# First two token pairs side by side, and the first attention products with their operand sums on GpSimd and TensorE's order written out

## The chip, the cores and the metric

The kernel runs on one core of one Trainium2 chip. The time is the device time of one execution in microseconds (us), lower is better; the kernel before took 1184.9 us in the median of three runs (1184.69 to 1185.73). The engines go by the profile's names: PE is TensorE (matmuls; PEld are its weight loads), DVE is VectorE, ACT is ScalarE, POOL is GpSimd, SP is the engine that issues the DMAs.

## The reference

The reference is one transformer layer on 1024 tokens (4 sequences of 256) of 512 features, all in float32:

```python
x = x + 0.5 * ffn(layernorm(x), A, B, Wr)
x = x + attn(layernorm(x), wq, wkv, wo)
x = x + 0.5 * ffn(layernorm(x), A, B, Wr)

# ffn: 64 experts of rank 16, gated by the softmax of the 16 best scores
scores = xf @ Wr.T
top_vals, top_idx = jax.lax.top_k(scores, 16)
h = jnp.einsum('nd,krd->nkr', xf, A)
out = jnp.einsum('nkr,kdr->nd', h * G[:, :, None], B)
# attn: 32 heads of width 128, causal
scores = jnp.einsum('bqhd,bkhd->bhqk', q[..., :128], k) * 192 ** -0.5
attn = jnp.einsum('bhqk,bkhd->bqhd', softmax(masked(scores)), v)
```

## The kernel before

Every large product is cut into 2 x 2 blocks and done with seven block products where plain multiplication has eight (Strassen-Winograd). The left and the right operands are first summed: `left_sums` (lines 166 to 175) and `right_sums` (177 to 187) make four sums each. `seven` (189 to 198) runs the products M1 to M7 in the order of a list, `STEPS` or `STEPS_LATE` (143 to 159). Several products add up in one PSUM bank, and after each product `read` takes a bank's state out, by ACT (a copy) or by DVE (an add). A product that adds to a bank waits until the earlier state has been read.

**First layer** (`ffn`, lines 239 to 431). It works on four pairs of 128-token tiles. A pair is prepared in three steps (`prepare`, 276 to 310): normalise (DVE statistics L103, ACT L106 to L120); transpose on PE (L127), copy out on ACT (L285) and sum on DVE (L171 to L174); the router's scores on PE (L302) and the gates on DVE and ACT (L249 to L273). Then come seven hidden products on PE (L318, one pair of 128x512 matmuls each, in the trace four instructions), the gating on POOL (`gated`, L345), the transposes of the gated result (`turned`, L364) and seven products back (L384) that DVE adds to `x` (L396). The right operand of the hidden products is the expert matrix A, which comes by DMA in four blocks; M1, M2 and M3 take raw blocks, M5 a sum of DVE (L181), M6 another of DVE (L184), M7 and M4 the sums of POOL (L185, L186). Pair 0 runs `STEPS_LATE`, which puts the raw blocks first. Pair 1 is prepared while pair 0's products run.

**Attention.** Its Q, K and V products use the scheme twice, an outer and an inner level: 7 x 7 = 49 products. The operand `xop[:, outer, inner]` (line 445) holds the normalised, transposed tokens and all their sums. `norm_pair` (457 to 489) fills outer blocks 0 and 1 from pairs 0 and 1, and the raw parts of 2 to 6 from pairs 2 and 3; `inner_sums` (450 to 456) makes the four inner sums of an outer block, each 128x256. The weights' sums are made on POOL by `two_levels` (505 to 535); two of them, `t3` and `t4` (L518, L521, 128x896), turn the sums for the outer M1 and M2 into those for M7 and M4, and may run only after the last matmul that reads the old ones. A *stage* is one outer product or two at a time: seven inner steps on PE (L607 for Q and K, `pqk_*`; L696 for V, `pv_*`), with eight read-outs, by ACT (L627, L727) or by DVE (L625, L637, L645, L721).

For the first head pair, `make_qk(0)` (lines 594 to 675) and the first V stages (`v_stages`, 685 to 766) run as follows: lines 898 to 915 take V and Q/K steps in turn, stage M1, then M2, then V's M6 with a Q/K stage of M6 and M5 together; between them the last token pair's part of `norm_pair` is taken, and the inner sums of outer blocks 5, 4 and 3 go to DVE, those of 2 and 6 to POOL. A memset of POOL (L664) clears a buffer of Q/K ahead. Then the loop over head pairs runs (from line 946): a *unit* is one head and one sequence: scores on PE (`ps`, L834, L835), masking and least value on DVE (L843), exponentials on ACT (L854), DVE (L862), ACT (L864), and one unit later the transposes (L875) and the product with V (L880, L887). The strings `FIRST_UNITS` to `LAST_UNITS` (line 942 on) say which steps are taken behind each unit's scores: `f` of the first Q/K, `g` of the first V stages, `q` of the next head pair's Q/K, `v` of V, `b` the rest of the unit before.

**What sets the order.** Instructions are traced in the order of the Python code; a scheduler then lays out each engine's queue at compile time, from that order as a priority and from when it takes operands to be ready. [...] `tc.keep_in_program_order(i)` holds an instruction behind everything traced before it on its engine. The DMAs of SP go in the order of its queue.

## Time and profile before

| what | value |
|---|---|
| three timed runs, median | 1184.9 us |
| the profiled execution, its own time | 1187.66 us |
| its span, first to last instruction | 1185.5 us |
| PE busy | 1166.3 us, 98% of the span, 6492 matmuls |
| DVE, ACT, POOL busy | 741.7, 492.7, 676.3 us |
| PE busy in 0 to 20 us | 17.18 us |
| PE busy in 20 to 36 us, granted clock | 14.25 us, 0.89 |
| PE busy in 130 to 150 us, granted clock | 17.68 us, 1.00 |
| PE busy in 150 to 166 us, granted clock | 9.90 us, 0.79 |
| PE busy in 176 to 400 us, granted clock | 224.00 us, 1.00 |

The first layer covers 0 to about 130 us, the attention about 130 to 1066 us, the second feed-forward layer the rest. A row of the timeline has its start, its duration, the engine, the source line, the operation, output<-input and the number of instructions merged; square brackets give the idle time ahead and what ended it. A row of the waits names the engine and line that waited, what it waited for, the total in us, the number of times and the longest. A float32 matmul of the program shows as two instructions. Busy time of PE is modelled at its ends, so a loss of PE is better read from the starts of its instructions: at full clock they follow each other every 0.43 us for 128x512, 0.215 us for 128x256 and 0.11 us for 128x128.

### The profile page before, as it was taken

The numbers are of one execution on the slowest core, as the hardware profiler recorded it, in microseconds if no ns is written. First come the engines' busy times: TensorE is split into PE (matmuls) and PEld (weight loads), VectorE is DVE, ScalarE is ACT, GpSimd is POOL, SyncE is SP. The second block draws the span as 40 slices with busy tenths as digits, with TensorE's granted clock in tenths as the row PEclk, the third lists the DMA queues.
The fourth block names the chain that finished last, engine by engine and source line by source line (L and its number), as shares of the span: only waits on it lengthen the run. The fifth ranks groups of instructions, "written<-read, shape, count | busy, mean of one in ns | idle before, by whom it ended". The sixth has DMA issues, their size and how long they took to land.

```text
span 1185.5 us, 18545 instructions
## 1 busy us (share of the span) xinstructions
PE 1166.3 (98%) x6492; PEld 1005.8 (85%) x6492; DVE 741.7 (63%) x1932; ACT 492.7 (42%) x1364; POOL 676.3 (57%) x933
## 2 busy tenths in 40 slices
PE   8999979999999999999999999999999999999998
PEld 5677869999999999999999898989898988875767
DVE  5444786566666666666576657665766666675432
ACT  4443314534443444344434443444443444546420
POOL 5611666986847684667575757657575644361110
PEclk9999989999999999999999999999999999999999
DMA  7001111111001101110111011110201000400001
GB/s 253 1 1 36 45 36 46 28 45 47 27 28 49 50 19 45 37 45 19 46 37 46 28 36 37 45 46 18 63 23 41 19 27 1 161 1 1 19 18 35
DMA packets 64940, 47.46 MB, mean 40 GB/s; under 512 B 4432, under 2 KB 55632, under 8 KB 64848
## 3 DMA queue, kind: packets, MB, share of 16 engines
q1 hardware_dynamic: 64848, 46.28, 13.2%
q8 instruction: 51, 0.84, 0.3%
q14 instruction: 41, 0.34, 0.1%
HBM read 44.17 MB, written 2.10 MB: 39 GB/s over the span
## 4 chain that ended last, share of the span: by engine, by line
PE 95%; DVE 2%; DMA 1%; ACT 1%; issue 0%; POOL 0%; SPq 0%; DVEq 0%; ACTq 0%
PE po L812 16%; PE pqk_c L607 8%; PE po_f L384 8%; PE pqk_a L607 8%; PE pqk_b L607 8%; PE ph_f L318 7%; PE pa L880 5%; PE ps L835 5%; PE pv_c L696 4%; PE pqk_d L607 4%; PE pv_b L696 4%; PE ptp L875 4%; PE ps L834 2%; PE pa L887 2%; PE pv_a L696 2%; PE pv_d L696 2%
## 5 line engine op out<-in xcount | busy, mean ns | idle before, releaser
L824 DVE TENSOR_TENSOR x<-x,po 128x512 f32<-128x512 f32 x224 | 153.9, 688 | 73.6 <-PE po L812 71.4
L854 ACT ACTIVATE s<-s,least 128x128 f32<-128x128 f32 (+1 forms) x256 | 114.5, 448 | 89.7 <-DVE least L843 89.7
L877 ACT COPY pT<-ptp 128x384 f32<-128x384 f32 x128 | 61.3, 479 | 207.6 <-PE ptp L875 207.6
L654 POOL TENSOR_TENSOR qk<-qk 128x256 f32<-128x256 f32 x128 | 92.7, 728 | 67.7 <-DVE qk L645 34.0
L864 ACT ACTIVATE s<-s,arden 128x128 f32<-128x128 f32 (+1 forms) x256 | 102.5, 448 | 51.5 <-DVE arden L862 51.2
L607 PE MATMUL pqk_a<-xop,wqk_M 128*128 128x256 f32 x448 | 116.9, 385 | 0.0
L607 PE MATMUL pqk_c<-xop,wqk_M 128*128 128x256 f32 x448 | 114.3, 381 | 0.0
L843 DVE CUSTOM_DVE_ANT_0 s<-ps,mask 128x128 f32<-128x128 f32 (+1 forms) x256 | 81.5, 356 | 51.0 <-PE ps L835 50.9
L345 POOL TENSOR_TENSOR hg_f<-hg_f,gate_f 128x512 f32<-128x512 f32 x32 | 33.6, 1057 | 132.1 <-DVE hg_f L331 68.9
L607 PE MATMUL pqk_b<-xop,wqk_M 128*128 128x256 f32 x420 | 106.9, 380 | 0.0
L645 DVE TENSOR_TENSOR qk<-qk,pqk_c 128x512 f32<-128x512 f32 x112 | 76.9, 688 | 43.0 <-PE pqk_c L607 33.8
L607 PEld LDWEIGHTS pqk_c<-xop,wqk_M 128*128 128x128 f32 x448 | 81.1, 191 | 9.7 <-DVE qk L645 1.0
L637 DVE TENSOR_TENSOR qk<-qk,pqk_b 128x512 f32<-128x512 f32 x105 | 72.2, 687 | 25.1 <-PE pqk_b L607 24.8
L181 POOL TENSOR_TENSOR wo<-wo 128x256 f32<-128x256 f32 x16 | 11.7, 728 | 128.0 <-DMA wo<-in_wo 112.6
L607 PEld LDWEIGHTS pqk_a<-xop,wqk_M 128*128 128x128 f32 x448 | 78.7, 194 | 6.5
L894 ACT COPY attn<-pa 128x256 f32<-128x256 f32 x128 | 47.5, 371 | 87.5 <-PE pa L887 87.5
L607 PEld LDWEIGHTS pqk_b<-xop,wqk_M 128*128 128x128 f32 x420 | 72.9, 191 | 6.1
L835 PE MATMUL ps<-qk 128*128 128x256 f32 x256 | 76.5, 381 | 0.0
L880 PE MATMUL pa<-pT,vbuf 128*128 128x256 f32 x256 | 76.2, 379 | 0.0
L812 PE MATMUL po<-wo,so 128*128 128x256 f32 x256 | 66.8, 383 | 1.7 <-DVE so L171 1.7
L812 PE MATMUL po<-to,attn 128*128 128x256 f32 x256 | 66.2, 381 | 0.9 <-DVE x L824 0.9
L607 PE MATMUL pqk_d<-xop,wqk_M 128*128 128x256 f32 x224 | 66.3, 380 | 0.0
(193 smaller groups left out, 2784.0 us busy)
## 6 DMA issues: line engine op xcount, KB each, us to landing
wv_M<-in_wkv SPq DMA_DIRECT2D x64, 128.0 KB, 2.5
wqk_M<-in_wq SPq DMA_DIRECT2D x64, 128.0 KB, 2.3
wqk_M<-in_wkv SPq DMA_DIRECT2D x64, 128.0 KB, 2.4
wo<-in_wo SPq DMA_DIRECT2D x16, 512.0 KB, 4.1
a_f<-in_a_t SPq DMA_DIRECT2D x8, 512.0 KB, 6.5
b_f<-in_b_t SPq DMA_DIRECT2D x4, 1024.0 KB, 8.8
x<-in_x SPq DMA_DIRECT2D x8, 256.0 KB, 8.2
out_x<-x SPq DMA_DIRECT2D x16, 128.0 KB, 1.7
```

Of the source, the lines that this page charges most:

```text
L318: nc.tensor.matmul(ps, lhsT=left[m][:, c, :], rhs=a_right[m][:, c, :], start=first and c == 0, stop=c == 1, skip_group_check=True,)
L384: nc.tensor.matmul(ps[:, 0:256], lhsT=left[m][:, c, :], rhs=b_right[m][:, c, :], start=first and c == 0, stop=c == 3, skip_group_check=True,)
L607: nc.tensor.matmul(ps[:, i * S : (i + 1) * S], lhsT=right[m][n], rhs=xop[:, OUTER[m], INNER[n]], start=first and i == 0, stop=True, skip_g ...
L654: nc.gpsimd.tensor_tensor(to, a, b, ALU.add)
L696: nc.tensor.matmul(ps[:, i * S + t * P : i * S + (t + 1) * P], lhsT=xop[:, OUTER[m], INNER[n], t * P : (t + 1) * P], rhs=right[m][n], star ...
L812: nc.tensor.matmul(ps[:, tt * 256 : (tt + 1) * 256], lhsT=outs[p][m][:, (2 * u + tt) * P : (2 * u + tt + 1) * P], rhs=right[m], start=firs ...
L824: nc.vector.tensor_tensor(to, to, ps.rearrange("p (t d) -> p t d", t=2), ALU.add)
L835: nc.tensor.matmul(ps[:, P : 3 * P], lhsT=qT[:, P : 2 * P], rhs=kT, start=True, stop=True)
L843: nc.vector.tensor_tensor_reduce(out=s[:, cols], in0=ps[:, cols], in1=mask_f[:, cols], scale=-SCALE, scalar=-TAKEN, op0=ALU.add, op1=ALU.m ...
L854: nc.scalar.activation(s[:, cols], s[:, cols], AF.Exp, bias=least[:, i : i + 1], scale=-1.0, accum_out=den[:, i : i + 1],)
L864: nc.scalar.mul(s[:, cols], s[:, cols], rden[:, i : i + 1])
L880: nc.tensor.matmul(po[:, 0 : 2 * P], lhsT=v_of(p, j, 2 * b), rhs=pT[:, 0 : 2 * P], start=True, stop=False,)
```

## The change

Seven edits, all before 200 us of the program:

1. The DMAs of the first layer: token tiles 2 and 3 are loaded between the second and the third block of A, tiles 4 to 7 behind the fourth (before: all six behind the fourth).
2. Pair 1 of the first layer is normalised, transposed and takes its first three hidden products ahead of pair 0's last four; both pairs use `STEPS_LATE`, pair 1 with M6 ahead of M5. POOL's sums of B are traced ahead of the gating of pair 0, and the gating of pairs 0 and 1 is pinned in program order.
3. POOL's sums of the first V weights are pinned behind the gating of pair 1 (`aside`).
4. The statistics of the last token pair are taken after two steps of the first V and Q/K stages, its transposes after seven.
5. All inner sums of outer blocks 2 to 6 and the last outer sums (before: two DVE adds, L484 and L485) go to POOL, pinned, in a fixed order with `t3` and `t4`.
6. The first Q/K: stages M1, M2, M6, then M4 with M7, M5 and M3. No memset of POOL.
7. From the first Q/K stage to the end of head pair 0, PE's queue is in the order of the code (`manual_schedule`), with new `FIRST_UNITS`.

The diff, cut to its core; left out are the arguments that pass `pinned` on to `two_levels`, `right_sums` and `left_sums`, and the returned instructions of `t3` and `t4`.

```diff
@@ -220,11 +228,11 @@
...
-        for kn in ((0, 0), (1, 0), (1, 1), (0, 1)):
+        for i, kn in enumerate(((0, 0), (1, 0), (1, 1), (0, 1))):
             c, e = a_block(*kn)
             nc.sync.dma_start(a_sb[:, c, e], a_v[:, c, e])
-        if between is not None:
-            between()
+            if between is not None and i % 2:
+                between(i // 2)
         for k in range(2):
@@ -334,20 +343,22 @@
...
-                steps = STEPS_LATE if late and pair == pairs[0] else STEPS
+                steps = STEPS_LATE if late and pair in pairs[:2] else STEPS
+                if late and pair == pairs[1]:
+                    steps = [steps[i] for i in (0, 1, 2, 4, 3, 5, 6)]
                 yield from seven(product, read, f"ph_{n}", steps)
-            def gated(hg, gate):
+            def gated(hg, gate, pinned):
                 ek = E // 2
...
                         to = hg[:, i, j * 512 : (j + 1) * 512].rearrange("p (e r) -> p e r", r=R)
-                        nc.gpsimd.tensor_tensor(
-                            to,
-                            to,
-                            gate[i][:, j * ek : (j + 1) * ek].unsqueeze(2).to_broadcast([P, ek, R]),
-                            ALU.mult,
+                        of = gate[i][:, j * ek : (j + 1) * ek].unsqueeze(2)
+                        made = nc.gpsimd.tensor_tensor(
+                            to, to, of.to_broadcast([P, ek, R]), ALU.mult
                         )
+                        if pinned:
+                            tc.keep_in_program_order(made)
@@ -402,13 +413,30 @@
...
             yield
-            take(tokens, 2)
+            take(tokens, 1)
+            if late:
+                second = prepare(pairs[1])
+                take(second, 1)
+            take(tokens, 1)
             a_right = a_sums()
             for u in range(n + 1):
-                hid = hidden(pairs[u], lefts[u], hgs) if u < n else iter(())
+                if u == 1 and late:
+                    hid = ahead
+                else:
+                    hid = hidden(pairs[u], lefts[u], hgs) if u < n else iter(())
                 tokens = prepare(pairs[u + 1]) if u + 1 < n else iter(())
                 behind = after(work, pairs[u - 2]) if u > 1 else iter(())
-                take(hid, 1)
+                if u == 0 and late:
+                    take(hid, 3)
+                    take(second, 1)
+                    ahead = hidden(pairs[1], lefts[1], hgs)
+                    take(ahead, 3)
+                    take(hid, 1)
+                    take(second, 1)
+                    tokens = iter(())
+                else:
+                    take(hid, 1)
                 take(behind, 1)
@@ -420,14 +448,17 @@
...
                 take(hid, 3)
-                if u < n:
-                    gated(hgs[pairs[u]], gated_by[u])
                 if u == 0:
                     b_right = b_sums()
+                if u < n:
+                    gated(hgs[pairs[u]], gated_by[u], late and u < 2)
+                if u == 1 and aside is not None:
+                    aside()
                 if u > 0:
...
                     take(steps, 8)
+        yield
         yield from after(None, pairs[n - 1])
@@ -447,12 +478,19 @@
...
-    def inner_sums(lo, hi, eng):
+    def inner_sums(lo, hi, eng, between=None):
         o = slice(lo, hi)
...
             blocks[2] = early
-        left_sums(eng, [xop[:, o, i] for i in (4, 5, 6, 2)], *blocks)
+        left_sums(eng, [xop[:, o, i] for i in (4, 5, 6, 2)], *blocks, pinned=lo > 0, between=between)
+    def last_outer():
+        for of, i in ((early[:, 1], 2), (xop[:, 1, 3], 3)):
+            tc.keep_in_program_order(
+                nc.gpsimd.tensor_tensor(xop[:, 6, i], of, xop[:, 5, i], ALU.subtract)
+            )
@@ -480,15 +518,12 @@
...
                 nc.scalar.copy(xop[:, 0:2, sl, cols], pt)
-        if half and a:
-            nc.vector.tensor_tensor(xop[:, 6, 2], early[:, 1], xop[:, 5, 2], ALU.subtract)
-            nc.vector.tensor_tensor(xop[:, 6, 3], xop[:, 1, 3], xop[:, 5, 3], ALU.subtract)
-        elif half:
+        if half and not a:
             nc.vector.tensor_tensor(xop[:, 6, sl], xop[:, 1, sl], xop[:, 5, sl], ALU.subtract)
-        elif a:
+        elif a and not half:
             inner_sums(0, 2, nc.vector)
-    raw, rights, outs = {}, {}, {}
+    raw, rights, outs, turns = {}, {}, {}, {}
@@ -557,15 +595,25 @@
...
                 ],
+                k == 1,
             )
+    def sums_v(k, pinned=False):
+        rights["v", k] = raw["v", k](**({"pinned": True} if pinned else {}))
+        return rights["v", k]
...
         experts = load_experts(
-            scope, "f1", "right", nc.vector, lambda: load_x(range(2, NT))
+            scope, "f1", "right", nc.vector, lambda i: load_x(range(4, NT) if i else (2, 3))
         )
...
         first_layer = ffn(
-            "f1", [(t, t + 1) for t in range(0, NT, 2)], *experts, after=norm_pair, late=True
+            "f1",
+            [(t, t + 1) for t in range(0, NT, 2)],
+            *experts,
+            after=norm_pair,
+            late=True,
+            aside=lambda: sums_v(0, True),
         )
@@ -642,10 +691,22 @@
...
                 to = part(blocks, r)
-                nc.vector.tensor_tensor(to, to, ps, ALU.add)
+                of = ps if ps.shape == to.shape else ps.to_broadcast(to.shape)
+                nc.vector.tensor_tensor(to, to, of, ALU.add)
                 done(r, into)
...
             return read
+        def m47(r, ps):
+            both, one, two, base = (part(slice(*k), r) for k in ((1, 3), (1, 2), (2, 3), (3, 4)))
+            if READS[r][2]:
+                nc.vector.tensor_tensor(both, both, ps, ALU.add)
+            else:
+                nc.scalar.copy(one, ps[:, 0:1])
+                nc.vector.tensor_tensor(two, base, ps[:, 1:2], ALU.add)
+            if r in LAST:
+                nc.gpsimd.tensor_tensor(one, one, two, ALU.add)
@@ -660,13 +721,16 @@
...
         else:
-            nc.gpsimd.memset(dst[:, 2], 0.0)
-            yield from stage(("M1",), fresh(slice(1, 2)), "m")
-            t3()
-            yield from stage(("M2",), branch(slice(0, 1)), "n")
-            t4()
-            yield from stage(("M6", "M5"), onto(slice(1, 3), 3), "a")
+            turns["qk"] = t3, t4
+            yield from stage(("M1",), fresh(slice(3, 4)), "m")
+            yield from stage(("M2",), branch(slice(0, 1), of=slice(3, 4)), "n")
+            yield from stage(("M6",), onto(slice(3, 4)), "o")
+            yield from stage(("M4", "M7"), m47, "r")
+            yield from stage(("M5",), onto(slice(2, 4)), "s")
+            load_qk(p + 1)
+            yield from stage(("M3",), onto(slice(3, 4)), "u")
+            return
         yield from stage(("M7", "M3"), onto(slice(1, 4, 2), 2), "c")
@@ -895,24 +962,31 @@
...
     load_qk(0)
+    written_out = ExitStack()
+    written_out.enter_context(tc.manual_schedule(engines={mybir.EngineType.PE}))
     first_qk = make_qk(0)
     first_v = chain(*(v_by[0][m] for m in ("M1", "M2", "M6", "M4M7")))
-    for _ in range(7):
-        take(first_v, 1)
-        take(first_qk, 1)
+    def first_products(n):
+        for _ in range(n):
+            take(first_v, 1)
+            take(first_qk, 1)
+    first_products(2)
     take(first_layer, 1)
-    for _ in range(7):
-        take(first_v, 1)
-        take(first_qk, 1)
-    inner_sums(5, 6, nc.vector)
-    inner_sums(4, 5, nc.vector)
+    first_products(5)
+    take(first_layer, 1)
+    tc.keep_in_program_order(turns["v"][0]())
+    tc.keep_in_program_order(turns["qk"][0]())
+    first_products(7)
+    inner_sums(5, 6, nc.gpsimd, last_outer)
+    tc.keep_in_program_order(turns["v"][1]())
     inner_sums(2, 3, nc.gpsimd)
+    inner_sums(3, 4, nc.gpsimd)
+    tc.keep_in_program_order(turns["qk"][1]())
+    inner_sums(4, 5, nc.gpsimd)
     inner_sums(6, 7, nc.gpsimd)
-    for _ in range(7):
-        take(first_v, 1)
-        take(first_qk, 1)
-    inner_sums(3, 4, nc.vector)
-    take(first_qk, 7)
+    first_products(7)
@@ -939,7 +1013,16 @@
...
     )
-    FIRST_UNITS = ("gfgfbgf", "gfgfbgfgf", "gvqvqbvqvq", "vqvqbvqvqvq", "vqvqbvqvqvq", "vqvqbvqq", "vqvqbqvqq", "vqvqbvqqq")
+    FIRST_UNITS = (
+        "gggg",
+        "gggfffbfffffvfvfvfv",
+        "fvfvfvbfvfvfvf",
+        "fvfvbfvfv",
+        "qqvqbqqvq",
+        "qqvqbqqvq",
+        "qqvqbqqvq",
+        "qqvqbqqvq",
+    )
     LAST_UNITS = ("", "b", "oob", "oob", "oob", "oob", "ooob", "ooob")
@@ -977,6 +1060,7 @@
...
             take(streams[k], 100)
+        written_out.close()
         sums_o(p)
```

More of the change, by code (lines that the diff above doesn't have):

```diff
@@ L164, in macaron_kernel, with left_sums @@
     LAST = (3, 4, 5, 6)
-    def left_sums(eng, s, a11, a12, a21, a22, *of):
+    def left_sums(eng, s, a11, a12, a21, a22, *of, pinned=False, between=None):
         s3 = s[3] if len(s) > 3 else a21
         r11, r12, r21, r22 = of or (a11, a12, a21, a22)
-        eng.tensor_tensor(s[0], r21, r22, ALU.add)
-        eng.tensor_tensor(s[1], s[0], r11, ALU.subtract)
-        eng.tensor_tensor(s[2], r12, s[1], ALU.subtract)
-        eng.tensor_tensor(s3, r11, r21, ALU.subtract)
+        for to, a, b, op in (
+            (s[0], r21, r22, ALU.add),
+            (s[1], s[0], r11, ALU.subtract),
+            (s[2], r12, s[1], ALU.subtract),
+            (s3, r11, r21, ALU.subtract),
+        ):
+            if to is s3 and between is not None:
+                between()
+            made = eng.tensor_tensor(to, a, b, op)
+            if pinned:
+                tc.keep_in_program_order(made)
         return {"M1": a11, "M2": a12, "M3": s[2], "M4": a22, "M5": s[0], "M6": s[1], "M7": s3}
@@ L237, in load_experts, with ffn @@
         )
-    def ffn(name, pairs, a_sums, b_sums, after, late):
+    def ffn(name, pairs, a_sums, b_sums, after, late, aside=None):
         with ExitStack() as scope:
@@ L344, in gated @@
                         to = hg[:, i, j * 512 : (j + 1) * 512].rearrange("p (e r) -> p e r", r=R)
-                        nc.gpsimd.tensor_tensor(
-                            to,
-                            to,
-                            gate[i][:, j * ek : (j + 1) * ek].unsqueeze(2).to_broadcast([P, ek, R]),
-                            ALU.mult,
-                        )
+                        of = gate[i][:, j * ek : (j + 1) * ek].unsqueeze(2)
+                        made = nc.gpsimd.tensor_tensor(
+                            to, to, of.to_broadcast([P, ek, R]), ALU.mult
+                        )
+                        if pinned:
+                            tc.keep_in_program_order(made)
             def turned(pair, hg):
@@ L503, in sums_o, with two_levels @@
         rights["o", p] = right_sums(nc.gpsimd, [t[:, i, :] for i in range(3)], *b, pinned=p == 0)
-    def two_levels(pool, bufs, name, blocks):
+    def two_levels(pool, bufs, name, blocks, pinned):
         t = {
@@ L517, in t3, with sums @@
         def t3():
-            nc.gpsimd.tensor_tensor(t["M1"], t["M6"], t["M1"], ALU.subtract)
+            return nc.gpsimd.tensor_tensor(t["M1"], t["M6"], t["M1"], ALU.subtract)
         def t4():
-            nc.gpsimd.tensor_tensor(t["M2"], t["M2"], t["M6"], ALU.subtract)
-        def sums():
+            return nc.gpsimd.tensor_tensor(t["M2"], t["M2"], t["M6"], ALU.subtract)
+        def sums(pinned=pinned):
             plain = {m: v[:, 0:4] for m, v in t.items()}
-            nc.gpsimd.tensor_tensor(plain["M5"], plain["M5"], plain["M1"], ALU.subtract)
+            first = nc.gpsimd.tensor_tensor(plain["M5"], plain["M5"], plain["M1"], ALU.subtract)
+            if pinned:
+                tc.keep_in_program_order(first)
             nc.gpsimd.tensor_tensor(plain["M6"], plain["M3"], plain["M5"], ALU.subtract)
@@ L547, in load_qk @@
                 ],
+                p == 1,
             )()
@@ L629, in fresh, with branch @@
             return read
-        def branch(blocks, into=None):
+        def branch(blocks, into=None, of=slice(1, 2)):
+            base = of
             def read(r, ps):
                 to = part(blocks, r)
-                of = to if READS[r][2] else part(slice(1, 2), r).to_broadcast(to.shape)
+                of = to if READS[r][2] else part(base, r).to_broadcast(to.shape)
                 nc.vector.tensor_tensor(to, of, ps, ALU.add)
@@ L688, in v_stages @@
             return {}
-        right, t3, t4 = raw["v", k]()
+        right, t3, t4 = rights.get(("v", k)) or sums_v(k)
         u = 2 + 2 * (k % 2)
+        if k == 0:
+            turns["v"] = t3, t4
+            t3 = t4 = None
         def stage(ms, read, name, behind=None):
```

## The prediction

> **What bounds the kernel now.** First the page's busy row and its slices: is one engine the limit, and where is it not?
>
> ```profile
> PE 1166.3 (98%) x6492; PEld 1005.8 (85%) x6492; DVE 741.7 (63%) x1932; ACT 492.7 (42%) x1364; POOL 676.3 (57%) x933
> ...
> PE   8999979999999999999999999999999999999998
> ```
>
> TensorE is the limit almost everywhere, and the change removes no matmul. So it can only give back time in which PE stands still or runs slowly, which is in the first slice and in slices 5 and 6 (118 to 178 us). Second, the waits of PE over the whole span (engine, line <- what it waited for: us, times, longest):
>
> ```profile
> PE pv_o L696 <- DVE vbuf L721: 6.1, 1, 6.1
> PE pth_f L364 <- POOL hg_f L345: 2.5, 1, 2.5
> ...
> PE pv_n L696 <- DVE vbuf L721: 1.4, 1, 1.4
> ...
> PE pv_a L696 <- ACT vbuf L727: 0.9, 2, 0.5
> ```
>
> These four rows lie in what the change touches. Third, the timeline around the two long ones. At the front:
>
> ```profile
> 17.33 1.88 PE L318 MATMUL ph_f<-at_f,fxs_f 128*128 128x512 f32 x4
> ...
> 20.63 1.06 POOL L345 TENSOR_TENSOR hg_f<-hg_f,gate_f 128x512 f32<-128x512 f32 x1
> ...
> 21.75 0.84 PE L364 MATMUL pth_f<-ident,hg_f 128*128 128x128 f32 x4 [2.54 <-POOL hg_f L345]
> ...
> 22.39 3.43 PE L318 MATMUL ph_f<-at_f,fxs_f 128*128 128x512 f32 x4
> ```
>
> PE has a transpose in its queue that waits for POOL's gating, which stands behind POOL's sums of A (L185 and L186, 16.01 to 20.67); pair 0's next product (M7, its operand made by L185 at 18.37) waits behind it. After the wait four instructions take 3.43 us where four took 1.88: the clock is halved. At the opening of the attention:
>
> ```profile
> 150.84 2.25 POOL L521 TENSOR_TENSOR wv_M<-wv_M,wv_M 128x896 f32<-128x896 f32 x1
> 151.08 2.29 DVE L173 TENSOR_TENSOR xop<-xop 128x256 f32<-128x256 f32 x1
> 153.05 2.24 POOL L521 TENSOR_TENSOR wqk_M<-wqk_M,wqk_M 128x896 f32<-128x896 f32 x1
> 153.29 2.29 DVE L172 TENSOR_TENSOR xop<-xop 128x256 f32<-128x256 f32 x1
> ...
> 156.17 0.41 DVE L721 TENSOR_TENSOR vbuf<-vbuf,pv_o 128x256 f32<-128x256 f32 x1
> ...
> 156.64 1.22 PE L696 MATMUL pv_o<-wv_M,xop 128*128 128x128 f32 x4 [6.10 <-DVE vbuf L721]
> ```
>
> DVE's inner sums take 0.41 us when alone (the ones at 155.50 and 155.84) and 2.29 beside POOL's `t4`; the read-out that PE needs stands behind five of them.
>
> **What there is to gain.** I add up, for each stretch, the distances between PE's starts less the usual distance of the shape (0.429, 0.2155 and 0.11 us for 128x512, 128x256 and 128x128). Front: 2.7 for the gap and about 1.65 for the half clock behind it, 4.35. 130 to 150 us: 3.2 (0.63, 0.62, 1.56 and crumbs). 150 to 166: 9.0 (a gap of 6.3; the rest is half clock until about 160.7). 166 to 176: 0.5. Together 17.0; in 176 to 400 the same sum is only 0.5. So the floor is 1185.5 - 17.0 = 1168.5 of span. The profiled execution took 1187.66, 2.16 more than its span and 2.76 more than the median of the runs; I take differences from the median, 1184.9, so the floor is 1167.9.
>
> **The change, part by part.**
>
> *Loads.* Two token tiles of 256 KB go ahead of the last two blocks of A. From 10 to 20 us the DMAs move 389 GB/s, so those blocks land 0.5 MB / 389 GB/s = 1.3 us later; DVE's L181, which waited for one at 13.24, starts near 14.6, L184 ends near 17.1, POOL's L185 near 19.5 and L186 near 21.8 (durations of before: 1.23, 1.21, 2.36, 2.35). M3 may start up to 1 us late if its block lands after 13.9. Behind them the same bytes have moved as before, so B is where it was when POOL took it without a wait at 21.64: nothing.
>
> *Two pairs side by side.* New work between 15.6 (end of pair 0's M3) and M7: pair 1's M1 to M3, 12 x 0.43 = 5.2 us. Its tokens should land near 12; statistics 1.7, then ACT's table load 1.28, square root to bias about 1.2, two L120 of 0.8: normalised near 16.3, transposes and copies 1 us: M1 near 17. M3 needs the left sums, and here is the price: DVE had 8.92 busy of 10 us from 10 to 20 before, and now takes pair 1's statistics (1.7) and left sums (1.65) into the same stretch. I expect PE idle for 1.5 us in all (bounds: none, and the whole 4.35 again if pair 1 comes so late that the clock halves). Behind it M5, M6, M7 and M4 find their operands made. Gain 4.35 - 1.5 = 2.9.
>
> *POOL's order at the front.* B's sums (four of 2.36) ahead of pair 0's gating (four of 1.06) end it near 21.8 + 9.4 + 4.2 = 35.5. Pair 0's transposes come after 14 products, two transposed pairs and two router passes, near 40. Nothing, under 4 us of cover; without it each us late is a us of PE. V's weight sums (11 us of POOL) move behind pair 1's gating, and are needed at 127: nothing.
>
> *The last token pair.* Its pinned statistics now queue behind the read-outs of two steps each: started 1.5 us later, so the second normalised tile is there 6.6 us behind the first product; PE's transposes stand behind 14 steps of 0.44, 6.1 us, and the second tile is turned from 7.0 on. Nothing, with 0.4 us of cover.
>
> *The memset.* Gone: 0.96 us of POOL, and the 11.42 us that POOL stood idle before it, since it waited for the buffer's former user. The Q/K weights' sums can then end near 120 instead of 129.5. With steps of V and Q/K in turn from the start, the 1.25 us lost at 130.6 and 131.8 should mostly go; ACT's two L120 of 0.8 still hold up copies. I leave 0.7.
>
> *Inner sums.* DVE loses 12 sums and 2 outer ones (0.33 apart when alone, 4.6 us; in the trace some 13, with the stretched ones). POOL gets them, at 0.69 from start to start (the rows of 144 to 147) where DVE has 0.33. Its chain is 22 x 0.69 + 4 x 2.15 = 23.8 us. It starts when DVE has read out the last pair, about 11.5 us behind the first product, and ends near 35. PE needs from it: the last sum for M6 at 17.4 (made at 15.8), M7's third step at 22.7 (made at 22.2), Q/K's M4 at 28.3 (25.8), M5 at 35 (28.7), M3 later than 42 (31.6 plus up to 3 for the head sums on POOL). It just fits, with 0.5 us at the narrowest. The Trainium skill's "GPSIMD Engine Reference" (4.1 Engine selection) speaks against this edit: elementwise sums of two tensors belong on VectorE, GpSimd being about twice as slow. The row agrees on the price (0.69 against 0.33), and by the rule the edit would cost 14 x 0.36 = 5 us. But its row is for an engine alone; here the sums on DVE cost 6.3 us of PE because they met POOL's. "SBUF — State Buffer" (Who interferes with whom) says what I rest on instead: a DVE instruction with two SBUF inputs contends with a GpSimd one that reads SBUF, one with a single SBUF input does not. Rows: L173 2.29 beside L521; L721 and L637, which read PSUM, 0.41 beside L518 at 142 to 144. By this the 5 us of POOL lie beside PE's work.
>
> *Q/K's stages.* The same matmuls. DVE's read-outs go from 20 x 0.41 + 16 x 0.69 = 19.2 to 32 x 0.41 + 12 x 0.69 = 21.4 us. In M2 and M6 each pair of steps brings 16 adds, 16 x 0.33 = 5.3 us per 6.1 of PE; with the last pair's ten sums on top DVE runs about 1 us behind, and an accumulating product waits for it, since only 1.3 us of PE lie between two uses of a bank. I leave 1.2 us of PE there (bounds: 0, and 4, half of what this place lost before).
>
> *Units in written order.* PE cannot pull other work forward any more. Behind unit 0's scores lie four steps of 0.88, 3.5 us; the chain to the probabilities took from 176.95 to 179.91 at unit 1 before, 3.0. Units 2 and 3 have 4 us and more. I leave 1.0 (bounds: 0, and 3).
>
> Attention: of 3.2 + 9.0 + 0.5 = 12.7 us, 0.7 + 1.2 + 1.0 stay, 9.8 are gained. With the front's 2.9 the sum is, by chance, 12.7 again: 1184.9 - 12.7 = 1172.2 (in a profiled execution 1187.66 - 12.7 = 1175.0). No wait over 2.5 us should be left, so no half clock.
>
> **Rivals.**
> *A. Only the attention gains.* For: PE's order in the first layer is not written out, and DVE is nearly full from 10 to 20 us. Then a gap moves instead of closing: 1184.9 - 9.8 = 1175.1.
> *B. DVE becomes the bound of the opening.* For: 87% load in M2 and M6. Against: the sums that stretched are gone. Half of the 9.8 stays: 1184.9 - 2.9 - 4.9 = 1177.1.
> *C. Nothing is left:* 1168.
> *D. Slower: POOL's pinned chain is late.* One queue of 23.8 us, each of whose members waits in order, with PE in a fixed order behind it. Beyond the 0.5 to 1.6 us of slack each us late is a us of PE, plus some 2 of half clock. To eat up the gain of 12.7 us and 2.4 more it would have to be 15 us late: sums of 1.2 us instead of 0.69, or a start at 26 instead of 11.5. The slowest such row is 0.90, beside DVE's own sums, which are gone. If so: 1188.
>
> **How the numbers follow.** The forecast 0.52, A 0.15, B 0.18, C 0.05, D 0.07, and 0.03 for a loss that just eats the gain. Measurement tells 0.2%, 2.4 us, from no change: faster 0.90, same 0.03, slower 0.07. The forecast's own bounds give 1168 to 1176; with A and B the range is 1167.5 to 1179.5, which leaves out D and the worst of B.
>
> **What would show it.** In the waits of PE the row L721 of 6.1 is gone and none exceeds 2; the granted clock from 147 to 163 is 1.00 where it was 0.79; no DVE row of 2.29; POOL without a gap for some 24 us; PE's gap ahead of L364 near 20 us gone. Wrong: PE waiting for `xop` or a weight's `t3`/`t4` (D), for DVE's read-outs by more than 2 us (B), a new gap near 16 to 20 us (A).

## The result and the profile after

The changed kernel takes 1176.46 us in the median of four runs (1175.92 to 1177.03), against 1184.8 us for the kernel before beside it (four runs, 1184.33 to 1185.73): a ratio of 0.9927, 95% interval 0.9915 to 0.994. It is faster by some 8.3 us, where the prediction had 12.7. The profiled execution after took 1176.84 us, with a span of 1175.1 us.

The page after, busy row and slices (tenths of each of 40 slices of 29.4 us):

```profile
PE 1162.9 (99%) x6492; PEld 1001.7 (85%) x6492; DVE 733.4 (62%) x1927; ACT 490.8 (42%) x1365; POOL 681.5 (58%) x942
...
PE   8999999999999999999999999999999999999998
PEclk9999999999999999999999999999999999999999
```

The dip around 150 us is gone and no slice runs at a lower clock. PE has the same 6492 matmuls; its busy time is 3.4 us less, since before some of them ran at half clock. The waits of PE after, whole span:

```profile
PE po L879 <- DVE so L180: 1.8, 1, 1.8
...
PE ph_f L327 <- DVE gate_f L277: 1.2, 1, 1.2
...
PE po_f L395 <- ACT hgT_f L376: 0.8, 1, 0.8
PE pv_c L763 <- DVE vbuf L788: 0.4, 1, 0.4
PE pqk_s L655 <- DVE qk L695: 0.4, 1, 0.4
PE pqk_n L655 <- DVE qk L686: 0.4, 1, 0.4
PE pv_n L763 <- DVE vbuf L788: 0.3, 1, 0.3
```

The wait of 6.1 us for the read-out is gone (L721 of before is L788 here), and none that exceeds 0.4 has come for it in the attention's opening. The first row is near the end of the attention, 900 us away from the change. In the first layer the wait of `pth_f` for POOL (2.5 before) is gone, but two rows are new: `ph_f` 1.2 and `po_f` 0.8. The timeline at the opening of the attention, POOL's queue:

```profile
134.34 2.11 POOL L553 TENSOR_TENSOR wv_M<-wv_M,wv_M 128x896 f32<-128x896 f32 x1 [16.75 <-PE pv_a L763]
136.38 2.11 POOL L553 TENSOR_TENSOR wqk_M<-wqk_M,wqk_M 128x896 f32<-128x896 f32 x1
...
143.49 2.08 POOL L556 TENSOR_TENSOR wv_M<-wv_M,wv_M 128x896 f32<-128x896 f32 x1
145.53 6.00 POOL L180 TENSOR_TENSOR xop<-xop 128x256 f32<-128x256 f32 x8
151.49 2.08 POOL L556 TENSOR_TENSOR wqk_M<-wqk_M,wqk_M 128x896 f32<-128x896 f32 x1
153.54 6.00 POOL L180 TENSOR_TENSOR xop<-xop 128x256 f32<-128x256 f32 x8
```

and two of DVE's read-outs beside the `t4` of 143.49:

```profile
144.28 0.42 DVE L788 TENSOR_TENSOR vbuf<-vbuf,pv_o 128x256 f32<-128x256 f32 x1
144.71 0.42 DVE L695 TENSOR_TENSOR qk<-qk,pqk_o 128x256 f32<-128x256 f32 x1
```

POOL works from 134.34 to 159.5 without a gap, and the read-outs, which take one input from PSUM, keep their 0.42 us beside it. Before, sums of two SBUF inputs took 2.29 there. Two stretches side by side show the clock (columns: stretch, its length, busy time and instructions of each engine, granted clock, DMA share, GB/s), first the kernel after:

```profile
147.00:163.00 16.00, 15.52 (x105) 13.85 (x103) 9.61 (x27) 6.84 (x21) 15.45 (x22) 1.00 0.25 67
```

and the kernel before, profiled a second time (the first experiment below):

```profile
147.00:163.00 16.00, 9.91 (x43) 8.40 (x42) 13.12 (x19) 0.00 (x0) 7.21 (x6) 0.68 0.00 0
```

To see where the time came from I add up PE's starts less the usual distances, as the prediction did, for both kernels (us lost in each stretch):

| stretch, us | before, first profile | before, second profile | after |
|---|---|---|---|
| 0 to 20 | 6.33 | 5.11 | 4.83 |
| 20 to 36 | 1.90 | 0.56 | 0.00 |
| 36 to 60 | -0.06 | -0.04 | 1.39 |
| 124 to 150 | 3.22 | 9.49 | 1.30 |
| 150 to 166 | 8.99 | 3.28 | 1.49 |
| 166 to 220 | 0.58 | 0.44 | 1.55 |
| 124 to 220 together | 12.79 | 13.21 | 4.34 |

(In the second profile the opening begins some 2.5 us earlier, so the same gap falls into another row.) The attention gives 8.9 us against the second profile. The first 60 us give nothing: 5.63 lost before, 6.22 after.

### The profile page after: what moved, and what is told of

The parts are those of the page before. It is cut to its first block, busy times and chain, and to the rows that moved or that the text cites. A ratio compares the mean times of both kernels' runs of the same rounds, so it can differ in the third digit from the quotient of the medians.

```text
span 1175.1 us, 18545 instructions
## 1 busy us (share of the span) xinstructions
PE 1162.9 (99%) x6492; PEld 1001.7 (85%) x6492; DVE 733.4 (62%) x1927; ACT 490.8 (42%) x1365; POOL 681.5 (58%) x942
## 4 chain that ended last, share of the span: by engine, by line
PE 96%; DVE 1%; ACT 1%; DMA 1%; SPq 0%; issue 0%; DVEq 0%; ACTq 0%
PE po L879 16%; PE po_f L395 8%; PE pqk_a L655 8%; PE pqk_c L655 8%; PE pqk_b L655 8%; PE ph_f L327 8%; PE ps L902 5%; PE pa L947 5%; PE pv_c L763 4%; PE pqk_d L655 4%; PE pv_b L763 4%; PE ptp L942 4%; PE ps L901 2%; PE pa L954 2%; PE pv_e L763 2%; PE pv_d L763 2%
## 5 line engine op out<-in xcount | busy, mean ns | idle before, releaser
L715 POOL TENSOR_TENSOR qk<-qk 128x256 f32<-128x256 f32 x120 | 87.1, 728 | 57.9 <-DVE qk L686 28.5
L655 PE MATMUL pqk_a<-xop,wqk_M 128*128 128x256 f32 x420 | 107.9, 380 | 0.0
L655 PE MATMUL pqk_c<-xop,wqk_M 128*128 128x256 f32 x420 | 107.1, 380 | 0.0
L695 DVE TENSOR_TENSOR qk<-qk,pqk_c 128x512 f32<-128x512 f32 x105 | 72.2, 688 | 41.0 <-PE pqk_c L655 32.0
L686 DVE TENSOR_TENSOR qk<-qk,pqk_b 128x512 f32<-128x512 f32 x105 | 72.2, 687 | 25.6 <-PE pqk_b L655 25.2
L655 PEld LDWEIGHTS pqk_c<-xop,wqk_M 128*128 128x128 f32 x420 | 76.1, 190 | 8.6 <-DVE qk L695 0.3
L655 PEld LDWEIGHTS pqk_a<-xop,wqk_M 128*128 128x128 f32 x420 | 72.5, 191 | 6.2 <-POOL wqk_M L192 0.3
L879 PE MATMUL po<-wo,attn 128*128 128x256 f32 x256 | 64.7, 379 | 0.0
```

The source lines that it names most:

```text
L655: nc.tensor.matmul(ps[:, i * S : (i + 1) * S], lhsT=right[m][n], rhs=xop[:, OUTER[m], INNER[n]], start=first and i == 0, stop=True, skip_g ...
L715: nc.gpsimd.tensor_tensor(to, a, b, ALU.add)
L879: nc.tensor.matmul(ps[:, tt * 256 : (tt + 1) * 256], lhsT=outs[p][m][:, (2 * u + tt) * P : (2 * u + tt + 1) * P], rhs=right[m], start=firs ...
```

## The experiments

Twelve kernels. "Before" beside the first four had a median of 1184.99 us, beside the next four 1185.38, beside the last four 1185.72; so between these groups the ratios compare better than the medians. A line number is that of each kernel's own code; in the rows shown the read-out of V is L721, L730, L786 or L788, `t4` is L521, L528, L554 or L556, and the inner sums are L171 to L174, L177 or L180.

| kernel | us, median | ratio to before, 95% interval |
|---|---|---|
| before again | 1185.69 (one run) | |
| front alone | 1184.69 | 0.9999 (0.9991 to 1.0007) |
| attention alone | 1176.9 | 0.9934 (0.992 to 0.9948) |
| before, sums on POOL | 1185.57 | 1.0005 (0.9997 to 1.0014) |
| after, sums on DVE | 1190.57 | 1.0041 (1.0028 to 1.0055) |
| after, PE's order not written | 1176.9 | 0.9928 (0.9916 to 0.9941) |
| after, POOL not pinned | 1185.48 | 1.0001 (0.9993 to 1.0009) |
| after, front mended | 1175.01 | 0.9912 (0.9899 to 0.9926) |
| before, sums on POOL and pinned | 1184.91 | 0.9994 (0.9988 to 1.0001) |
| front mended, M5 first | 1175.19 | 0.991 (0.9896 to 0.9923) |
| front mended, opening written | 1173.69 | 0.99 (0.9884 to 0.9916) |
| all of these | 1173.61 | 0.9894 (0.9881 to 0.9908) |

**Before again.** No edit.

> The kernel before, unchanged, profiled once more. My theory of why the gain by the medians (8.3 us) is smaller than the one between the two profiled executions (10.4 us of span): the profiled execution of before, 1187.66, was itself 2.8 us above its median, because the clock halved after both long waits, and in most executions it does so only after one of them or for a shorter time. Then this profile has the same two waits (2.5 and 6.1 us within 0.3) and a span between 1182.0 and 1184.0, with the half-clock stretch at 22 to 26 us or at 156 to 161 us missing or shorter. The rival, that every execution halves the clock at both places and the difference lies elsewhere, expects both stretches as they were and a span of 1185 or more.

Measured: 1185.69 us, span 1183.6. In kind as expected: one place at half clock, not two. In size a miss, since I had expected the waits within 0.3: at the front PE waited 1.4 us where the first profile has 2.5, and the clock stayed full behind it. The timeline of this second profile at the front:

```profile
17.11 2.35 POOL L186 TENSOR_TENSOR at_f<-a_f,at_f 128x1024 f32<-128x1024 f32 x1
19.42 1.06 POOL L345 TENSOR_TENSOR hg_f<-hg_f,gate_f 128x512 f32<-128x512 f32 x1
20.53 0.66 PE L364 MATMUL pth_f<-ident,hg_f 128*128 128x128 f32 x4 [1.37 <-POOL hg_f L345]
21.02 1.88 PE L318 MATMUL ph_f<-at_f,fxs_f 128*128 128x512 f32 x4
```

The gating starts at 19.42 instead of 20.63, because the last block of A was there earlier: DVE's L181 started at 12.03 instead of 13.24, with no wait ahead of it where it had stood 1.08 us for the block in the first profile, and the four instructions behind the wait take 1.88 us instead of 3.43. In five executions with the old load order this sum started at 13.24 (the profile that I predicted from), 12.03, 12.11, 12.01 and 12.26. So the front that I had read was the odd one of five: its 4.35 us of loss were 1.5 to 2.0 in the other four.

**Front alone.** Edits 1 to 3 on the kernel before (the changed lines of `load_experts`, `hidden`, `gated` and the loop of `ffn`, with `aside`); the attention as before.

> The kernel before with the edits of the first layer alone (loads, pairs 0 and 1 side by side, POOL's order with the V sums behind pair 1's gating). From the ledgers of the two profiles (8.2 us lost before 60 us in before, 6.2 in after) I expect 2.0 us less than before: 1182.8, between 1181.8 and 1184.0. The rival, that the front only moves its gap (1.35 us at 15 us and 1.0 at 44.6 us stand where 2.7 stood, and the half clock of before is not in most executions), expects 1184.0 to 1185.0.

Measured: 0.9999 (0.9991 to 1.0007). My theory's number is missed, the rival's is right: the front edits give nothing. Its losses (same sum) are 4.45 us up to 36 and 1.40 from 36 to 60, 5.85 together, against 5.63 of the second profile before.

**Attention alone.** Edits 4 to 7; the loads and the first layer as before.

> The kernel after with the first layer as it was before (loads, order of the pairs, gating and B sums, V sums not pinned), so the attention edits alone. My theory expects most of the gain here: 1178.5, between 1177.3 and 1179.5, the rest of the way to 1176.5 being the front's. The rival that the two parts need each other (the V sums out of POOL's way, for one) expects over 1180.

Measured: 0.9934 (0.992 to 0.9948), 8.1 us by the medians: nearly all of the result comes from here. The 1176.9 us are less than the 1177.3 to 1179.5 that I expected, since I still left 2 us to the front.

**Before, sums on POOL.** The inner sums of outer blocks 5, 4 and 3 and the two last outer sums to POOL, and nothing else:

```diff
...
-    inner_sums(5, 6, nc.vector)
-    inner_sums(4, 5, nc.vector)
+    inner_sums(5, 6, nc.gpsimd)
+    inner_sums(4, 5, nc.gpsimd)
...
-    inner_sums(3, 4, nc.vector)
+    inner_sums(3, 4, nc.gpsimd)
```

> The kernel before with one edit: the inner sums of outer blocks 3, 4 and 5 and the two last outer sums on POOL instead of DVE, in the old places of the code; PE's order is the scheduler's, Q/K's stages are the old ones. My theory (the 6 us gap comes from DVE's sums stretched beside POOL's, and goes with them) expects 1178 to 1181, without a DVE row over 1 us in the opening. The rival (the written order of PE and of POOL makes the gain; sums moved alone only make POOL late, 14 x 0.69 = 10 us more in its queue) expects 1184 or more, with PE waiting for xop.

Measured: 1.0005 (0.9997 to 1.0014). My theory fell here, and the rival's number held: the wait of 6.1 us for L721 is gone, and as much has come for it (4.4, 1.2 and 0.9 us). PE's waits and POOL's queue in this kernel:

```profile
PE pqk_c L607 <- DVE qk L645: 4.4, 1, 4.4
...
PE pv_o L696 <- POOL xop L172: 1.2, 1, 1.2
```

```profile
156.75 2.08 POOL L521 TENSOR_TENSOR wv_M<-wv_M,wv_M 128x896 f32<-128x896 f32 x1
158.78 2.07 POOL L521 TENSOR_TENSOR wqk_M<-wqk_M,wqk_M 128x896 f32<-128x896 f32 x1
160.80 2.78 POOL L654 TENSOR_TENSOR qk<-qk 128x256 f32<-128x256 f32 x4
```

Unpinned, both `t4` stand behind all inner sums, and behind them Q/K's head sums (L654), for which DVE waits 4.68 us, and PE for DVE.

**After, sums on DVE.** The reverse: the kernel after with those sums back on DVE; the pins of what is left on POOL and PE's written order are kept.

```diff
...
-    inner_sums(5, 6, nc.gpsimd, last_outer)
+    inner_sums(5, 6, nc.vector, last_outer)
+    inner_sums(4, 5, nc.vector)
...
-    inner_sums(3, 4, nc.gpsimd)
...
-    inner_sums(4, 5, nc.gpsimd)
...
+    inner_sums(3, 4, nc.vector)
```

> The kernel after, with the inner sums of outer blocks 5, 4 and 3 and the two last outer sums back on VectorE; t3, t4 and the sums of 2 and 6 stay pinned on GpSimd, TensorE's order stays written out. Collision theory (a VectorE sum with two SBUF inputs stretches from 0.41 to 2.3 us beside a GpSimd one, and the read-outs stand behind it): the sums meet t3, t4 and the GpSimd sums, rows of L180 near or above 2 us come back, TensorE waits 4 to 8 us for a read-out between 145 and 165 us: 1180 to 1185 us. Rival, the order alone gained: VectorE does a sum in 0.33 us when alone, so the chain is even shorter: 1176 to 1177 us.

Measured: 1.0041 (1.0028 to 1.0055), 1190.57 us: slower than before, and worse than the 1180 to 1185 that the collision theory gave. DVE, POOL and PE in it:

```profile
142.36 1.64 DVE L180 TENSOR_TENSOR xop<-xop 128x256 f32<-128x256 f32 x1
143.92 0.94 DVE L491 TENSOR_TENSOR xop<-xop 128x256 f32<-128x256 f32 x1
```

```profile
141.63 2.08 POOL L554 TENSOR_TENSOR wv_M<-wv_M,wv_M 128x896 f32<-128x896 f32 x1 [3.39 <-PE pv_n L761]
143.68 3.49 POOL L180 TENSOR_TENSOR xop<-xop 128x256 f32<-128x256 f32 x4
```

```profile
150.90 1.22 PE L761 MATMUL pv_o<-wv_M,xop 128*128 128x128 f32 x4 [7.16 <-DVE vbuf L786]
```

A DVE sum takes 1.64 us beside `t4` and 0.94 beside POOL's small sums. These slow down too: four take 3.49 us here, 0.87 each, where eight took 6.00 in the kernel after, 0.75 each. PE waits 7.16 for the read-out behind them. The collision is shown, on both engines.

**After, PE's order not written.** One line out; POOL's pins stay.

```diff
-    written_out.enter_context(tc.manual_schedule(engines={mybir.EngineType.PE}))
```

> The kernel after without the written order of TensorE's queue; the pins on GpSimd stay. Theory one, GpSimd's place and order are what counts, and TensorE's queue comes out nearly as written because the trace order is its priority: within 1 us of the kernel after, 1176.5 to 1177.5. Rival, the written order is an equal part (moving the sums alone gave nothing): the scheduler puts steps early that wait for VectorE or GpSimd, excess of 3 us and more between 130 and 180 us, 1179 to 1184.

Measured: 0.9928 (0.9916 to 0.9941), the ratio of the kernel after. The written order gives nothing in sum. It isn't without effect: without it the losses are 2.9 us in 124 to 150 (1.3 with it) and 1.56 in 150 to 220 (3.04 with it).

**After, POOL not pinned.** PE's order stays written:

```diff
-        left_sums(eng, [xop[:, o, i] for i in (4, 5, 6, 2)], *blocks, pinned=lo > 0, between=between)
+        left_sums(eng, [xop[:, o, i] for i in (4, 5, 6, 2)], *blocks, between=between)
...
-    tc.keep_in_program_order(turns["v"][1]())
+    turns["v"][1]()
```

and so for `t3`, for Q/K and for the outer sums.

> The kernel after without the pins of t3, t4, the inner sums and the last outer sums on GpSimd; TensorE's order stays written out. Theory one, the pinned order is needed: without it t4 drifts behind all inner sums, as it did where only the sums were moved (t4s at 156.8 to 160.8 us), and TensorE in its fixed order waits for it 3 to 6 us: 1179 to 1184. Rival, the stages' order and TensorE's written order do it alone: 1176 to 1177.5.

Measured: 1.0001 (0.9993 to 1.0009). Without the pins the whole gain is gone, more than the 1179 to 1184 us that I expected. POOL's queue and PE in it:

```profile
146.47 8.26 POOL L180 TENSOR_TENSOR xop<-xop 128x256 f32<-128x256 f32 x12
154.69 2.07 POOL L554 TENSOR_TENSOR wv_M<-wv_M,wv_M 128x896 f32<-128x896 f32 x1
```

```profile
156.82 1.43 PE L761 MATMUL pv_c<-wv_M,xop 128*128 128x128 f32 x5 [5.31 <-POOL wv_M L554]
```

V's `t4` comes at 154.69 instead of 143.49, and PE waits for it.

**Before, sums on POOL and pinned.** The kernel before with POOL's sums in the pinned order, the stages of Q/K, the time of the last pair and PE's order as before:

```diff
...
-    inner_sums(5, 6, nc.vector)
-    inner_sums(4, 5, nc.vector)
-    inner_sums(2, 3, nc.gpsimd)
-    inner_sums(6, 7, nc.gpsimd)
+    inner_sums(5, 6, nc.gpsimd)
+    inner_sums(4, 5, nc.gpsimd)
+    tc.keep_in_program_order(turns["v"][1]())
+    inner_sums(2, 3, nc.gpsimd)
+    inner_sums(3, 4, nc.gpsimd)
+    tc.keep_in_program_order(turns["qk"][1]())
+    inner_sums(6, 7, nc.gpsimd)
```

> The kernel before with two things only: the inner sums of outer blocks 5, 4 and 3 and the last outer sums on GpSimd, and GpSimd's order pinned (t3 of V and Q/K, outer sums, inner sums of 5, 4, t4 of V, 2, 3, t4 of Q/K, 6). First layer, stages of Q/K, times of the last pair and TensorE's order stay as before. Theory, place and pinned order of the sums are the gain (the sums alone gave nothing, the kernel after without pins gave nothing, the kernel after without TensorE's written order kept it all): the wait of 6 us goes and no wait over 2 us comes for it, 1177 to 1179.5. Rival, the new stages of Q/K and the earlier last pair are needed too, since the joint stage of M6 and M5 asks for the sums of blocks 5 and 4 at once (GpSimd has them by about 145, the stage starts near 143): TensorE waits for xop 2 to 4 us, 1180 to 1183.

Measured: 0.9994 (0.9988 to 1.0001). The theory that place and pins are all fell too; the rival was right that more is needed, though not about what, nor by how much (1180 to 1183 expected, 1184.91 found). The wait for `xop` is there with 1.6 us; the large one is another:

```profile
PE pqk_c L614 <- DVE qk L652: 5.9, 1, 5.9
...
PE pqk_a L614 <- POOL xop L177: 1.6, 1, 1.6
```

```profile
157.17 2.07 POOL L528 TENSOR_TENSOR wqk_M<-wqk_M,wqk_M 128x896 f32<-128x896 f32 x1
159.20 0.72 POOL L177 TENSOR_TENSOR xop<-xop 128x256 f32<-128x256 f32 x1
159.88 0.72 POOL L661 TENSOR_TENSOR qk<-qk 128x256 f32<-128x256 f32 x1
```

The old joint stage of M6 and M5 ends in head sums on POOL (L661), and these now stand at the end of POOL's chain; DVE stands idle 6.2 us for them. In the kernel after, Q/K's head sums run from 162.24 on, behind the chain, and no row of PE's waits leads to them.

**After, front mended.** Two edits of the front. The gate of the first tile is traced between DVE's two sums of A, both pinned; and the gates of pair 2 are traced behind pair 0's transposes, their exponentials pinned there:

```diff
...
+            tc.keep_in_program_order(first)
+            between()
+        second = eng.tensor_tensor(t[0], b22, b12, ALU.subtract)
+            tc.keep_in_program_order(second)
...
+                made = nc.scalar.activation(ex, sc, AF.Exp, bias=nmax)
+                if behind:
+                    tc.keep_in_program_order(made)
```

> The kernel after with two edits of the front. The gate of the first token tile is traced between VectorE's two sums of A, and the two are pinned, so that the first sum stands behind the reciprocal of pair 1 and the second behind the first gate (the gate freed a PSUM bank at 16.6 us that TensorE had waited for since 15.57). The gates of pair 2 are traced behind pair 0's transposes and their exponentials pinned behind the copies of these (the copies stood behind a table load and two exponentials until 44.74). Theory, the front's gain of 2.9 us was eaten by two new waits of 1.2 and 0.8 us: both go, 1176.5 - 2.0 = 1174.5. Rival, in the first layer a gap only moves, since ScalarE and VectorE are full there: new waits of the same sum, 1176 to 1177.

Measured: 0.9912 (0.9899 to 0.9926), 1.4 us under the kernel after by the medians; the intervals overlap. The losses from 36 to 60 fall from 1.39 to 0.41: the second mend works, as expected. Those up to 20 us stay (4.83 and 4.76): there the gap moved. And the reason that I had given for the first was wrong. The wait at 15.4 was not for a bank; PE had pair 0's M6 next, which takes DVE's second sum of A, and that ended at 16.61:

```profile
14.06 1.23 DVE L189 TENSOR_TENSOR a_f<-a_f 128x1024 f32<-128x1024 f32 x1 [1.18 <-DMA a_f<-in_a_t]
...
15.40 1.21 DVE L192 TENSOR_TENSOR at_f<-a_f 128x1024 f32<-128x1024 f32 x1
...
16.76 1.10 PE L327 MATMUL ph_f<-at_f,fxs_f 128*128 128x512 f32 x2 [1.19 <-DVE gate_f L277]
```

This is the timeline of the kernel after. The row of PE names L277, the DVE instruction that ended last; the operand on the same row, `at_f`, says what was needed.

**Front mended, M5 first.** Pair 0's M5, whose operand is ready, ahead of pair 1's transposes, and these pinned behind it: `take(hid, 3)` becomes `take(hid, 4)`, and the `take(hid, 1)` after pair 1's three products goes.

> The kernel with the front mended, and pair 0's M5 traced ahead of pair 1's transposes, which are pinned behind it. In the front mended TensorE had M3, transposes that waited for the normalised tokens (16.17), then M6 that waited for VectorE's second sum of A (17.54); M5's operand was there at 15.23. So the wait of the kernel after at 15.4 to 16.76 was for that second sum, not for a bank as I had put it. Theory: M5 covers both, 1.0 us less than the front mended (1175.0): 1174.0. Rival, another wait takes its place: 1174.7 to 1175.5.

Measured: 0.991 (0.9896 to 0.9923), no different from the front mended, as the rival had it. In its profile no gap over 0.25 us is left between 6 and 60 us, and the loss up to 36 is 3.94 instead of 4.76; but 0.55 is lost between 60 and 90, where the front mended lost none. The sum is 0.5 us in the spans (1173.0 and 1173.5), and the medians don't show it.

**Front mended, opening written.** PE's written order ends ahead of the first unit:

```diff
     first_products(7)
+    written_out.close()
...
-        written_out.close()
         sums_o(p)
```

> The kernel with the front mended, with TensorE's written order ended ahead of the first unit. Theory: the written order gains in the opening what it loses among the units (starts of TensorE less their usual distance, 124 to 150 us: 1.3 with the order written, 2.9 without; 150 to 220 us: 3.0 with, 1.6 without), so ending it between the two keeps both: about 1.0 to 1.4 us less than the front mended (1175.0): 1173.6 to 1174.0. Rival, the differences are those of single executions: 1175.0.

Measured: 0.99 (0.9884 to 0.9916), 1173.69 us, 1.3 under the front mended, as expected. The losses are 1.31 us in 124 to 150 and 1.76 in 150 to 220, where the profile of the front mended has 1.90 and 2.53. Of the first difference 0.59 is a gap of the units that begins at 149.6 there, so the opening is equal in both: it keeps what the written order gives, and the units get back most of what it costs.

**All of these.**

> Both of the two edits before together: front mended with M5 first, and the written order of TensorE ended ahead of the first unit. If both gain and add up 1173.0 (1172.5 to 1173.5); if neither does 1175.0.

Measured: 0.9894 (0.9881 to 0.9908), 1173.61 us: the opening's gain alone, M5 adds nothing that can be told. Beside the kernel with M5 first, from which it differs only by where the written order ends, it gains 1.6 us (1173.27 to 1173.69 against 1174.54 to 1176.59). It is the best version, 2.9 us under the kernel after by the medians. The largest wait of PE that is left in the attention's opening is one for POOL's `t4` (`PE pqk_r L671 <- POOL wqk_M L572: 0.6, 1, 0.6`).

## Why the prediction was right or wrong

1176.46 lies within the range, which the rivals A and B had widened, and 4.3 us above the forecast, just outside the forecast's own bounds (1168 to 1176). The direction and the mechanism of the attention held, with 8.1 us gained where I had 9.8; the front did not.

**What there is to gain: the step that failed.** I added up 4.35 us at the front in one profiled execution and took the gain from the median of the runs, which was 2.76 us shorter than that execution. Nearly all of those 2.76 us were this: in the second profile the front's gap is 1.5 instead of 2.7, and no half clock follows. The losses up to 36 us differ by 2.6 (8.23 and 5.67). So in an ordinary run the front had 1.5 us to give, and my own price for the new front, 1.5 us, ate all of it. With the right ledger the sum would have been 1184.9 - 9.8 = 1175.1, the number of rival A.

**Two pairs side by side.** I left 1.5 us of idle time; it was 1.35 at 15.4 us, since pair 0's M6 stood ahead of pair 1's products, which I had taken for its cover, and 1.0 at 44.85, which I had put at nothing "under 4 us of cover". That cover was POOL's; what came late was ACT's copy of the transposed gating (L376, 44.74), behind a table load at 42.95 and two exponentials. I had counted the new work on DVE, and not asked what ACT has in its queue when pair 2's gates fall into pair 0's transposes.

**Loads.** I said 1.3 us later for A's last block. DVE's sum of it started at 13.1 to 14.6 in the nine kernels with the new order (14.06 in the kernel after, forecast 14.6), against 12.0 to 12.3 in four of the five executions with the old: nearer 1.9. The second sum ended at 16.61 where I had 17.1, and it is what PE waited for.

**Start of M1.** 0.7 left by forecast, 0.0 found: the sum over 124 to 130 us is 0. **M2 and M6.** 1.2 left, 1.28 found between 130 and 140, as DVE's lag.

**POOL's chain.** It fits, but with less to spare than I had. From `t3` to the last inner sum it takes 25.2 us where I had 23.8: the 22 sums follow each other every 0.74 us in the mean, not 0.69, since the pinned order puts sums that need each other side by side (0.80 to 0.83 where a sum reads the one just before it, 0.69 elsewhere), and a sum for `wo` of 0.68, which I had not counted, stands among them. The chain starts with `t3` at 134.34, before the last pair is turned, so the sums end 31 us behind the first product, not 35. No row of PE's waits names `xop`, but one of its weight loads does, at the place where I had 0.5 us to spare (M7's third step):

```profile
151.90 1.19 PEld L763 LDWEIGHTS pv_c<-wv_M,xop 128*128 128x128 f32 x10 [0.59 <-POOL xop L180]
151.94 1.24 PE L763 MATMUL pv_c<-wv_M,xop 128*128 128x128 f32 x9 [0.43 <-DVE vbuf L788]
```

PE had finished the product before at 151.34. POOL's sum ended at 151.53, 0.2 us late, and DVE's read-out for the same product at 151.79, which hides it. Rival D is answered by its own test, and the experiments show how near it was: with the pins off, PE waits 5.3 us for one `t4`.

**Inner sums and the rule against them.** The "GPSIMD Engine Reference" of the Trainium skill (4.1 Engine selection) puts such sums on VectorE; that it means an engine alone, as the prediction has it, the page does not say. Followed in the kernel after, it gives 1190.57 us, 14 more. "SBUF — State Buffer" (Who interferes with whom) was the rule that decided: sums of two SBUF inputs 0.94 and 1.64 beside POOL, adds from PSUM 0.42.

**Units in written order.** 1.0 left by forecast; 3.0 found from 150 to 220 us. This term was mis-sized by 2 us. One part (0.6 at 151.3, the two rows above) is V's M4 with M7 taken alone, with nothing between its steps: the next product waits for DVE's L788, which waits for ACT's copy (L817). Another (0.6 at 171.3) is a DVE queue of 0.68 us adds for V and Q/K, one behind the other.

**What it does not do singly.** I had argued the move of the sums as the cause, with the rest as accompaniment. The runs show a set. Sums on POOL without pins (in the kernel before and in the kernel after), pins without the new stages, and everything without the move each give back all of the 8 us, and the wait changes its name: head sums (4.4), `t4` (5.3), head sums (5.9), the read-out (7.2). PE's written order is not one of the set. That the new stages are what was missing in the pinned kernel is read from its row L661, not tried by itself: that kernel also kept the old time of the last pair and POOL's memset.

## What to carry to other kernels

A ledger of losses belongs to one execution: before differences are taken from the median, ask which of its losses make that execution longer than the median, and take those off first. When work is moved to a second engine, list everything in that engine's queue that others wait for, and where it will stand: here `t4` and the head sums became late in turn, until order and stages were fixed together. An order written out by hand is worth ending where it stops paying; the opening gained 1.6 us by it and the units behind lost 1.5 (one profile with it, one without).

## What I had not expected of the hardware

The half clock comes in whole pieces. In the clock records of the fourteen profiles its stretches between the first and the last instruction were 3.41, 6.83, 10.24 and 13.65 us, all multiples of 3.41, and they last beyond the moment when PE is busy again. The kernel before in its second profile (one stretch of 10.24 us), then the kernel with the sums on DVE (one of 13.65); the columns are those of the two rows at the result:

```profile
150.10:160.20 10.10, 6.10 (x18) 5.24 (x19) 7.93 (x13) 0.00 (x0) 3.38 (x3) 0.50 0.00 0
```

```profile
145.80:159.40 13.60, 7.04 (x24) 6.14 (x25) 11.06 (x18) 0.00 (x0) 6.88 (x7) 0.50 0.00 0
```

The skill's "TensorE: Matmul & The Clock Gate" (Part 1) has a window of 3413 ns that runs freely and does not start with the kernel; the multiples agree, and so does the case of one gap with two outcomes. A gap of 1.95 us near 1041 us left the clock full in the kernel after, and was followed by 3.41 us of half clock in the profile of the attention alone. First the attention alone, then the kernel after:

```profile
1040.80:1044.10 3.30, 1.51 (x9) 1.02 (x8) 3.26 (x5) 0.48 (x1) 2.33 (x1) 1.00 0.00 0
1044.20:1047.50 3.30, 3.30 (x10) 2.66 (x9) 1.59 (x3) 1.66 (x2) 1.60 (x3) 0.50 0.00 0
```

```profile
1040.00:1043.40 3.40, 1.61 (x10) 1.13 (x8) 2.93 (x4) 0.85 (x2) 2.68 (x2) 1.00 0.00 0
1043.40:1046.80 3.40, 3.40 (x18) 2.73 (x17) 2.57 (x6) 1.66 (x2) 1.41 (x2) 1.00 0.00 0
```

The profile of the attention alone took 1178.34 us, 1.4 more than its median, with a mean clock of 0.999; its other four executions had 1.000. The same goes for the one execution at 0.999 of four other kernels (PE's order not written, the front mended, M5 first, the opening written): 1.2 to 2.0 us above the median of its kernel. So whether a gap of some 2 us costs only itself, or some 1.7 more (an estimate, half of 3.41), differs from execution to execution. In these profiles single gaps up to 1.8 never brought it, two of 1.34 and 1.06 us close together did, so did the one of 2.7 at the front of the first profile, and those of 4.6 and more always did.
